# Last layer of a four-layer megakernel: 32 rows per head in zeroed persistent buffers, and four bf16 products ahead of each score tile

## The chip, the core and the metric

The program runs on one core of a Trainium2 chip. A core has five engines with queues of their own: TensorE (PE; its weight loads are shown as PEld), VectorE (DVE), ScalarE (ACT), GpSimd (POOL) and SyncE (SP, which issues the DMAs here). TensorE writes to PSUM, which has eight banks of 128 partitions x 512 fp32; everything else lies in SBUF (128 partitions) or in device memory. Instructions of one engine run in the order in which they were queued; between engines they wait on semaphores.

The metric is the device time of one launch in microseconds (us), as the median of several runs. Before the change it is 3215.15 us over 3 runs (3209.72 to 3215.69).

## What is computed

Four layers follow each other on x of shape (4, 1024, 128). Each does `xn = layernorm(x); x = x + attention(xn) * silu(ffn(xn))`, each with another attention and another feed-forward part. The change touches the attention of the last layer alone: 16 heads of 8 columns, causal softmax attention with learned relative positions.

```python
qx, kx, vx = split_head(x @ Wq.T), split_head(x @ Wk.T), split_head(x @ Wv.T)
ex = rel_embed[ns].reshape(n, NH, HD).transpose(1, 0, 2)        # 256 rows
srel = srel_skew(einsum('bhnd,hmd->bhnm', qx, ex))
...
qk = (einsum('bhnd,bhmd->bhnm', qx, kx) + srel) * inv_dim
mask = 1000000000.0 * triu(ones((n, n)), 1)
atten = softmax(qk - mask, axis=-1)
out = einsum('bhnm,bhmd->bhnd', atten, vx)
return merged_heads(out) @ Wp.T + bp
```

A head has 8 columns, so each score is a sum over 8 products.

## The kernel before

Layers 0 to 2 take the first two thirds of the time and are not edited. The last layer (`layer3`, from line 1725) goes over 4 batches x 4 groups of 4 heads; a group is one pass over 8 query tiles of 128 tokens, in the order `ORDER3 = (7, 0, 6, 1, 5, 2, 4, 3)`. One query tile of one group is a *unit* (128 units). A unit of query tile t has (t+1) x 128 keys and is worked in *score tiles* of up to 512 keys for the 4 heads at once: one score tile when t <= 3, two when t > 3, so 12 a group and 192 in all.

**q and k of a group.** `project3` (line 1962) allocates q as [128, 1 + 1024] and k as [128, 1024] from a pool with two buffers each, sets column 0 of q to zero on POOL (line 1967), and loads the 8 rows of each of the 4 heads by DMA to partitions 32j to 32j+7 (line 1971). The other 24 partitions of each 32 hold nothing. A matrix product whose operands lie on partitions 32j and up uses the row group j of TensorE's array, so four heads lie in four row groups.

**Relative part.** `relative3` (line 1988) multiplies, for two of the four heads and two query tiles, 8 rows of q by 8 rows of the embedding `W["emb"]`, 256 columns wide (line 2000, `pr`). ACT copies the result from PSUM (line 2002, `r`), four DMAs write it to a table in device memory (`flat`, lines 2005 and 2006), and `shear3` (line 2009) reads it back shifted by one column a row (`rel`, lines 2021 to 2027). POOL sets the masked places by affine selects (line 2031). The products run up to seven units ahead of their use, the reads three.

**Scores.** `scores3` (line 2044) is a generator. It first queues the four products of a score tile (line 2064, `score`, one per head, 8 rows each, one PSUM bank each; the four banks are the only buffer of the tag "sc"), then on DVE the scaling, adding of `rel` and row minimum of each head (lines 2072 and 2079, with a read of the accumulator), and after the last score tile of a unit the exponential on ACT (line 2086).

**Weighted sum.** DVE transposes the weights in 32 x 32 blocks (line 1791, `wT`), and `weigh3` (line 2092) multiplies them with `vb`, the values of a group spread so that each of four key blocks has its 8 columns of 32 (line 2100, `po`: 128 rows, 32 columns, 64 or 32 wide, in a column group of the array per head).

**Order.** The main loop (lines 1823 to 1853) takes a turn per score tile, plus four at the end, 196 turns: queue the products of the next score tile, the transposes due, a third of a weighted sum, then DVE's work on the next score tile. At the end of a unit it adds the relative part of a later unit, the load of a later `rel`, a step of whatever lies beside (`ffn3`, the feed-forward part, in the second group of each batch; `begin3`, the layer norm and projections of the next batch, in the third), and at set places `project3` and the values of the next group. A scheduler may then move an instruction among its engine's others as its dependencies allow. PSUM is shared out as "sc" 1 buffer of 4 banks, "tr" 3 buffers of one bank (used by `pr`, the feed-forward part, the projections and transposes) and "o" 1.

fp32 products show as two records each in the profile, so a score tile has 8 MATMUL records.

The loop that the change adds to:

```python
        for x, (n, first) in enumerate(tiles + [(len(units), 0)] * 4):
            next(fill, None)
            if transposes and transposes[0][0] < x:
                transpose(*transposes.pop(0)[1:])
            step()
            next(fill, None)
```

Of the kernel before, what the change touches and what calls it, by code (L numbers as in the profile page):

```python
# [10 lines left out]
F32 = mybir.dt.float32  # L11
BF16 = mybir.dt.bfloat16
# [7 lines left out]
P = 128  # L20
NB = 4
T = 1024
# [65 lines left out]
def drain(gen):  # L88
    for _ in gen:
        pass  # L90
# [1634 lines left out]
def layer3(k, W, x3, out, eps5, ps, first):  # L1725

    nc, tc = k.nc, k.tc
    with ExitStack() as st:
        pool = lambda name, bufs, **kw: st.enter_context(tc.tile_pool(name=name, bufs=bufs, **kw))
        p1, p2, temp, dram = pool("l3", 1), pool("l3d", 2), pool("l3r", 3), pool("rel3", 6, space=DRAM)  # L1740
        vb = p1.tile([P, 32, 4, 4, 8], F32, tag="vb", name="vb")
        nc.gpsimd.memset(vb, 0.0)
        units = [(b, i, t) for b in range(NB) for i in range(4) for t in ORDER3]
        batch, group, flats, rels = {}, {}, {}, {}

        def part(h):

            at, h = divmod(h, 8)
            if at < 4 * NB:
                pair = ORDER3[h // 4 * 4 + h // 2 % 2] // 2  # L1750
                if h % 2 == 0:
                    flats[at, pair] = dram.tile([2, 4, P, 384], F32, tag="flat", name="flat")
                relative3(k, W, temp, ps, flats[at, pair], group[at]["q"], at % 4, pair, h % 2)

        def ahead(n):
            if n < len(units):
                t = units[n][2]
                rels[n] = shear3(k, p2 if t > 3 else p1, flats[n // 8, t // 2], t)

        def stream():  # L1760
            for n, (b, i, t) in enumerate(units):
                yield from scores3(k, p1, p2, ps, group[n // 8], rels.pop(n), t)

        batch[0] = {"qk": first["qk"], "vd": first["vd"], "xnT": p1.tile([P, T], F32, tag="xnT", name="xnT")}
        nc.sync.dma_start(out=batch[0]["xnT"], in_=first["xnT"])
        group[0] = {}
        drain(project3(k, p2, batch[0], 0, group[0]))
        drain(values3(k, p1, batch[0], vb, 0))
        for n in range(7):
            part(n)  # L1770
            if n in (1, 3):
                ahead(n // 2)
        ahead(2)
        beside, project, values = iter(()), iter(()), iter(())
        weights, transposes, weighs, out_of = {}, [], [], {}

        def transpose(n, heads):

            b, i, t = units[n]
            at, pair = n // 8, t // 2  # L1780
            big = t > 3
            if (at, pair) not in weights:
                for w in [w for w in weighs if w[0] == big]:
                    drain(w[1])
                    weighs.remove(w)
                weights[at, pair] = [
                    p1.tile([P, 2, 1024 if big else 512], F32, tag=f"w{'b' if big else 's'}{j}", name="wT") for j in range(4)
                ]
            S = group[at]["S", t]
            for j in heads:  # L1790
                nc.vector.transpose(weights[at, pair][j][:, t % 2, 0 : (t + 1) * P], S[j][:, 0 : (t + 1) * P])  # L1791
            if n % 8 in (2, 3, 6, 7) and heads[-1] == 3:
                weighs.append((big, weigh(n)))

        def weigh(n):
            nonlocal values
            b, i, t = units[n]
            at, pair = n // 8, t // 2
            if n % 8 == 2:
                out_of[at] = ps.tile([P, 8, 32], F32, tag="o", name="po")  # L1800
            o = out_of[at]
            yield from weigh3(k, weights.pop((at, pair)), vb, o, pair)
            if n % 8 == 7:
                drain(values)
                if i == 0:
                    batch[b]["on"] = p1.tile([P, 4, 256], F32, tag="on", name="on")
                finish3(k, p1, ps, o, group[at]["sums"], batch[b]["on"][:, i, :])
                if i == 3:
                    end3(k, W, temp, ps, x3, b, batch[b], out[b])
            yield  # L1810

        def step():

            while weighs:
                if next(weighs[0][1], weighs) is not weighs:
                    return
                weighs.pop(0)

        tiles = [(n, first) for n, (b, i, t) in enumerate(units) for first in range(0, (t + 1) * P, 512)]
        fill = stream()  # L1820
        next(fill)
        next(fill)
        for x, (n, first) in enumerate(tiles + [(len(units), 0)] * 4):
            next(fill, None)
            if transposes and transposes[0][0] < x:
                transpose(*transposes.pop(0)[1:])
            step()
            next(fill, None)
            last = n < len(units) and (x + 1 == len(tiles) or tiles[x + 1][0] > n)
            if not last:  # L1830
                continue
            b, i, t = units[n]
            at, pos = n // 8, n % 8
            transposes += [(x, n, heads) for heads in (((0, 1), (2, 3)) if t > 3 else ((0, 1, 2, 3),))]
            if pos == 0 and at + 1 < 4 * NB:
                group[at + 1] = {}
                project = project3(k, p2, batch[(at + 1) // 4], (at + 1) % 4, group[at + 1])
            if pos == 0 and i == 1:
                beside = ffn3(k, W, p1, temp, ps, batch[b])
            if pos == 3 and i == 2 and b + 1 < NB:  # L1840
                batch[b + 1] = {}
                beside = begin3(k, W, p1, p2, temp, ps, dram, x3, b + 1, eps5, batch[b + 1])
            if pos == 0:

                next(project, None)
            part(n + 7)
            if pos == 2:
                next(project, None)
            if pos == 6 and at + 1 < 4 * NB:
                values = values3(k, p1, batch[(at + 1) // 4], vb, (at + 1) % 4)  # L1850
                next(values)
            next(beside, None)
            ahead(n + 3)
        while weighs:
            step()
# [103 lines left out]
            yield  # L1959


def project3(k, p2, seq, i, group):

    nc = k.nc
    q = p2.tile([P, 1 + T], F32, tag="q", name="q")
    kk = p2.tile([P, T], F32, tag="k", name="k")
    nc.gpsimd.memset(q[:, 0:1], 0.0)
    group.update({"q": q, "k": kk, "sums": p2.tile([P, 4, NT], F32, tag="sums", name="sums")})
    for n, dst in ((0, q[:, 1:]), (1, kk)):
        for j in range(4):  # L1970
            nc.sync.dma_start(out=dst[32 * j : 32 * j + 8], in_=seq["qk"][n, 32 * i + 8 * j : 32 * i + 8 * j + 8])
        yield


def values3(k, p1, seq, vb, i):

    nc = k.nc
    v = p1.tile([P, 32, 32], F32, tag="vr", name="vr")
    for a in range(4):
        rows = slice(32 * a, 32 * a + 32)  # L1980
        nc.sync.dma_start(out=v[rows], in_=seq["vd"].rearrange("(n r) d -> r n d", r=32)[:, :, 32 * i : 32 * i + 32])
    yield
    for a in range(4):
        rows = slice(32 * a, 32 * a + 32)
        nc.gpsimd.tensor_copy(vb[rows, :, :, a, :], v[rows].rearrange("p n (j d) -> p n j d", d=8))


def relative3(k, W, temp, ps, flat, q, i, pair, jp):

    nc = k.nc
    r = temp.tile([P, 2, 2, 256], F32, tag="temp", name="r")
    js = (2 * jp, 2 * jp + 1)
    pr = [ps.tile([P, 2, 256], F32, tag="tr", name="pr") for _ in js]
    for m in range(2):
        for j, to in zip(js, pr):
            at, t = slice(32 * j, 32 * j + 8), 2 * pair + m
            nc.tensor.matmul(to[:, m, :], q[at, t * P : (t + 1) * P], W["emb"][at, i, :], start=True, stop=True)  # L2000
    for n, to in enumerate(pr):
        nc.scalar.copy(r[:, n], to)  # L2002
    rows = flat.rearrange("m j p u -> p j m u")
    for m in range(2):
        nc.sync.dma_start(out=rows[:, 2 * jp : 2 * jp + 2, m, 0:256], in_=r[:, :, m])
        nc.sync.dma_start(out=rows[:, 2 * jp : 2 * jp + 2, m, 256:384], in_=r[:, :, m, 0:P])
# [37 lines left out]
def scores3(k, p1, p2, ps, group, rel, t):  # L2044
# [5 lines left out]
    nc = k.nc  # L2050
    q, kk = group["q"], group["k"]
    n = (t + 1) * P
    at = lambda j: slice(32 * j, 32 * j + 8)
    size = "b" if t > 3 else "s"
    S = [(p2 if t > 3 else p1).tile([P, T if t > 3 else 512], F32, tag=f"S{size}{j}", name="neg") for j in range(4)]
    group["S", t] = S
# [3 lines left out]
    for first in range(0, n, 512):  # L2060
# [7 lines left out]
        for j in range(4):  # L2068

            neg, m = S[j], low[j]  # L2070
# [157 lines left out]
```

## Time and profile before

| | |
|---|---|
| time, median of 3 runs | 3215.15 us (3209.72 to 3215.69) |
| profiled execution, span | 3215.9 us, 50605 instructions |
| PE, DVE, ACT, POOL busy | 72%, 72%, 47%, 36% of the span |
| mean granted TensorE clock | 0.741 of full speed |
| the last layer's scores, `score` L2064 | 1536 records, mean 739 ns |
| products with the embedding, `pr` L2000 | 1024 records, mean 560 ns |
| weighted sums, `po` L2100 | 10240 records, mean 256 ns |
| DVE on the scores, L2079 with `low` / without, L2072 | 448 x 516 ns, 320 x 521 ns, 192 x 416 ns |
| DVE transposes, L1791 | 512 x 754 ns |
| exponentials on ACT, L2086 | 512 x 763 ns |
| copies of `pr` on ACT, L2002 | 256 x 581 ns |
| selects on `rel` on POOL, L2031 | 288 x 638 ns |

The page of the profile names a group of instructions by line, engine, operation and tiles, then its busy time, the mean duration of one, and the idle time of that engine just before them with what ended it. Its first rows give the busy share of the engines in 40 slices of the span, and below these the clock that was granted to TensorE, in tenths of full speed. The last layer lies in the last third of the slices. Matmuls are pipelined and their ends are modelled, so the duration of a single record includes time in which the next one already runs.

### The profile page before, as it was taken

To read this page: it belongs to the slowest core of one execution; us is meant where nothing else is said; L and a number is where in the kernel's file an instruction comes from. 1 tells how busy PE (TensorE), PEld (TensorE's weight loads), DVE (VectorE), ACT (ScalarE), POOL (GpSimd) and SP (SyncE) were. 2 spreads that over 40 slices of the span, in tenths; PEclk is the share of its full clock that TensorE was granted. 3 is DMA by queue.
4 is the path that set the end of the run, shared out by engine and by line. 5 is a ranking of instruction groups with operands and counts; after the bars stand their busy time and mean duration, and the time that the engine had idled before them with its cause. 6 is when DMAs were issued, how large, how long until landed. Compare 5 with 4: busy or idle time off the path is not lost. (4 is left out here: it accounts for less than half of the span.)

```text
span 3215.9 us, 50605 instructions
## 1 busy us (share of the span) xinstructions
PE 2305.2 (72%) x18321; PEld 1320.3 (41%) x18321; DVE 2300.9 (72%) x5538; ACT 1496.1 (47%) x3256; POOL 1155.9 (36%) x1100
## 2 busy tenths in 40 slices
PE   5787778577777766984443772477888888988985
PEld 2555556222232322661110232255555555555553
DVE  5555545878888886657777887547778688688686
ACT  3555544333333333435332561236655665665663
POOL 3334343134444444224468233232222322323322
PEclk9888888588878877995655675566766766767676
DMA  3000000100000000330333446257676677677672
GB/s 87 6 1 1 1 1 1 35 0 0 0 0 7 7 7 7 112 105 7 86 104 100 133 113 139 92 153 209 192 214 202 183 219 217 183 211 209 195 228 68
DMA packets 397310, 308.18 MB, mean 96 GB/s; under 512 B 96368, under 2 KB 379884, under 8 KB 391428
## 3 DMA queue, kind: packets, MB, share of 16 engines
q1 hardware_dynamic: 395908, 300.75, 32.9%
q10 hardware_dynamic: 1152, 4.19, 0.4%
q8 instruction: 144, 2.36, 0.3%
q14 instruction: 106, 0.87, 0.1%
HBM read 162.72 MB, written 141.56 MB: 95 GB/s over the span
## 5 line engine op out<-in xcount | busy, mean ns | idle before, releaser
L2086 ACT ACTIVATE neg<-neg,low 128x640 f32<-128x640 f32 (+7 forms) x512 | 390.0, 763 | 165.1 <-DVE low L2079 165.0
L2031 POOL TENSOR_SCALAR_AFFINE_SELECT rel<-rel 128x512 f32<-128x512 f32 x288 | 180.6, 638 | 577.4 <-DMA rel<-flat 366.4
L1791 DVE STREAM_TRANSPOSE wT<-neg 128x640 f32<-128x640 f32 (+7 forms) x512 | 362.9, 754 | 12.8 <-ACT neg L2086 9.3
L2064 PE MATMUL score<-k,q 8*128 8x512 f32 (+3 forms) x1536 | 294.0, 739 | 86.3 <-DVE low L2079 85.4
L2079 DVE CUSTOM_DVE_ANT_0 neg<-score,rel,low 128x128 f32<-128x128 f32 (+3 forms) x448 | 217.4, 516 | 153.8 <-issue 71.1
L2000 PE MATMUL pr<-emb,q 8*128 8x256 f32 x1024 | 243.9, 560 | 56.1 <-ACT r L2002 29.7
L2100 PE MATMUL po<-wT,vb 128*32 128x64 f32 (+1 forms) x10240 | 236.1, 256 | 35.4 <-issue 24.1
L2100 PEld LDWEIGHTS po<-wT,vb 128*32 128x32 f32 x10240 | 203.3, 138 | 140.3 <-issue 83.9
L2000 PEld LDWEIGHTS pr<-emb,q 8*128 8x128 f32 x1024 | 156.0, 266 | 137.4 <-ACT r L2002 65.7
L2002 ACT COPY r<-pr 128x512 f32<-128x512 f32 x256 | 136.9, 581 | 142.9 <-PE pr L2000 102.6
L2079 DVE CUSTOM_DVE_ANT_0 neg<-score,rel 128x512 f32<-128x512 f32 (+3 forms) x320 | 149.5, 521 | 24.1 <-PE score L2064 8.9
L2064 PEld LDWEIGHTS score<-k,q 8*128 8x128 f32 x1536 | 103.5, 248 | 146.4 <-DVE low L2079 110.5
L835 PE MATMUL pg<-xnT,w 128*128 128x512 f32 x256 | 148.1, 662 | 6.8 <-DVE h L839 3.2
L788 POOL TENSOR_TENSOR prod<-rest,kv 128x2048 f32<-128x2048 f32 x32 | 145.5, 4593 | 18.4 <-ACT rest L778 18.4
L826 PE MATMUL po<-h,w 128*128 128x512 f32 x256 | 131.5, 635 | 27.0 <-DVE h L839 27.0
L214 PE MATMUL pt<-ident,three 128*24 128x128 bf16 x64 | 9.2, 295 | 197.6 <-DVE three L211 197.6
L837 PE MATMUL pu<-xin,w 128*128 128x512 f32 x256 | 140.9, 634 | 13.7 <-DVE h L839 7.7
L838 ACT ACTIVATE h<-pg 128x512 f32<-128x512 f32 x128 | 75.9, 595 | 156.5 <-PE pg L835 153.1
L1084 PE MATMUL ph<-xin,upT 128*128 128x512 bf16 (+1 forms) x128 | 69.8, 575 | 65.3 <-DVE xin L1078 63.9
L431 PE MATMUL px<-hT,xbcT 128*128 128x512 f32 x256 | 115.4, 595 | 0.0
L1489 PE MATMUL read<-kt,const_sb 128*128 128x128 f32 x256 | 50.7, 370 | 90.2 <-POOL kt L1484 90.2
L2072 DVE TENSOR_SCALAR_CACHE_REDUCE neg<-score 128x384 f32<-128x384 f32 (+2 forms) x192 | 79.9, 416 | 47.7 <-PE score L2064 46.2
(631 smaller groups left out, 5671.7 us busy)
## 6 DMA issues: line engine op xcount, KB each, us to landing
flat<-r SPq DMA_DIRECT2D x256, 256.0 KB
rel<-flat SPq DMA_DIRECT2D x112, 512.0 KB
flat<-r SPq DMA_DIRECT2D x256, 128.0 KB
rel<-flat SPq DMA_DIRECT2D x96, 256.0 KB
kt<-kd SPq DMA_DIRECT2D x16, 512.0 KB
qt<-qd SPq DMA_DIRECT2D x16, 512.0 KB
kdc<-kdd SPq DMA_DIRECT2D x16, 512.0 KB
ktc<-ktd SPq DMA_DIRECT2D x16, 512.0 KB
```

The source lines that it names most:

```text
L788: nc.gpsimd.tensor_tensor(prod, attn.rearrange("p (t h g) -> p t h g", t=4, g=16)[:, t].unsqueeze(2).to_broadcast(each), kv[:, t, 1, :].re ...
L826: nc.tensor.matmul(po, W["w2"][:, e, c, :], h[:, c, :], start=(e == 0 and c == 0), stop=(e == 7 and c == 1))
L835: nc.tensor.matmul(pg, W["w1"][:, e, c * P : (c + 1) * P], xnT, start=True, stop=True)
L837: nc.tensor.matmul(pu, W["w3"][:, e, c * P : (c + 1) * P], xin, start=True, stop=True)
L1791: nc.vector.transpose(weights[at, pair][j][:, t % 2, 0 : (t + 1) * P], S[j][:, 0 : (t + 1) * P])
L2000: nc.tensor.matmul(to[:, m, :], q[at, t * P : (t + 1) * P], W["emb"][at, i, :], start=True, stop=True)
L2002: nc.scalar.copy(r[:, n], to)
L2031: nc.gpsimd.affine_select(out=rel[:, :, slot(back), :], in_=rel[:, :, slot(0), :], compare_op=op, fill=fill, base=0, pattern=[[0, 4], [-si ...
L2064: nc.tensor.matmul(sc[:, j, 0 : last - first], q[at(j), 1 + t * P : 1 + n], kk[at(j), first:last], start=True, stop=True)
L2079: nc.vector.tensor_tensor_reduce(out=neg[:, begin:last], in0=sc[:, j, begin - first : last - first], in1=rel[:, j, slot : slot + (last - b ...
L2086: nc.scalar.activation(neg[:, 0:n], neg[:, 0:n], AF.Exp, bias=here, scale=-1.0, accum_out=group["sums"][:, j, t : t + 1])
L2100: nc.tensor.matmul(o[32 * j : 32 * j + 32, 2 * pair + m.start : 2 * pair + 2, :], vb[:, kb, j].rearrange("p a d -> p (a d)"), weights[j][: ...
```

## The change

Three things change, all in the last layer.

First, q and k of the groups are no longer taken from a rotating pool. Two pairs of buffers are allocated once and set to zero as a whole, one pair on DVE and one on POOL, and a group uses the pair of its parity. `project3` loads the same 8 rows per head into them by the same DMAs, and its memset of q's first column is dropped, since that column stays zero.

Second, the products of `relative3` and `scores3` take 32 rows per head where they took 8. The 24 added rows of q and k are zero (those of `W["emb"]` are zero as well), so the sums stay what they were.

Third, at the start of each turn of the main loop `keep_warm(4)` queues four bf16 products of the identity (128 x 128, `k.ident16`) with a tile of ones (128 x 512) into one PSUM buffer of the tag "tr". Nothing reads the result. `tc.keep_in_program_order` marks them for the scheduler. In the order as built, a group of four stands ahead of nearly every score tile, some with products of `relative3` or part of a weighted sum between, and each of the four has a weight load of its own.

```diff
         p1, p2, temp, dram = pool("l3", 1), pool("l3d", 2), pool("l3r", 3), pool("rel3", 6, space=DRAM)
+        pairs = []
+        for n in range(2):
+            q, kk = p1.tile([P, 1 + T], F32, tag=f"q{n}", name="q"), p1.tile([P, T], F32, tag=f"k{n}", name="k")
+            for a in (q, kk):
+                (nc.gpsimd if n else nc.vector).memset(a, 0.0)
+            pairs.append((q, kk))
         vb = p1.tile([P, 32, 4, 4, 8], F32, tag="vb", name="vb")
+        ones = p1.tile([P, 512], BF16, tag="ones16", name="ones")
+        nc.vector.memset(ones, 1.0)
+
+        def keep_warm(count):
+
+            spare = ps.tile([P, 512], F32, tag="tr", name="spare")
+            for _ in range(count):
+                tc.keep_in_program_order(nc.tensor.matmul(spare, k.ident16, ones, start=True, stop=True))
+
...
-        drain(project3(k, p2, batch[0], 0, group[0]))
+        drain(project3(k, p2, pairs[0], batch[0], 0, group[0]))
...
         for x, (n, first) in enumerate(tiles + [(len(units), 0)] * 4):
+            keep_warm(4)
             next(fill, None)
...
-                project = project3(k, p2, batch[(at + 1) // 4], (at + 1) % 4, group[at + 1])
+                project = project3(k, p2, pairs[(at + 1) % 2], batch[(at + 1) // 4], (at + 1) % 4, group[at + 1])
...
-def project3(k, p2, seq, i, group):
+def project3(k, p2, pairs, seq, i, group):
 
     nc = k.nc
-    q = p2.tile([P, 1 + T], F32, tag="q", name="q")
-    kk = p2.tile([P, T], F32, tag="k", name="k")
-    nc.gpsimd.memset(q[:, 0:1], 0.0)
+    q, kk = pairs
...
         for j, to in zip(js, pr):
-            at, t = slice(32 * j, 32 * j + 8), 2 * pair + m
+            at, t = slice(32 * j, 32 * j + 32), 2 * pair + m
             nc.tensor.matmul(to[:, m, :], q[at, t * P : (t + 1) * P], W["emb"][at, i, :], start=True, stop=True)
...
-    at = lambda j: slice(32 * j, 32 * j + 8)
+    at = lambda j: slice(32 * j, 32 * j + 32)
```

## The prediction

> **What bounds the kernel now.** I read the stretch of the last layer first (busy time by window), then what VectorE (DVE) waits for in it, then single windows, because only the last layer is edited. The columns are the stretch in us, its length, busy us and instructions (x) of PE, PEld, DVE, ACT, POOL, then the granted TensorE clock, the DMA share and GB/s.
>
> ```profile
> 2173.00:3193.00 1020.00, 853.55 (x13084) 541.21 (x13088) 801.22 (x2526) 625.95 (x1476) 289.30 (x412) 0.69 0.69 198
> ```
>
> These are 1020 of the 3215.9 us. PE is busy 84% of them, DVE 79%, and the clock is 0.69, so TensorE does at a reduced rate what would take less at full rate. Neither engine is full; the two wait for each other. The waits of DVE in that stretch:
>
> ```profile
> DVE neg L2079 <- issue: 76.9, 28, 7.5
> DVE neg L2079 <- PE score L2064: 68.5, 51, 3.8
> DVE neg L2072 <- PE score L2064: 28.1, 14, 4.6
> DVE wT L1791 <- ACT neg L2086: 9.3, 19, 3.0
> DVE neg L2079 <- POOL rel L2031: 9.2, 4, 4.6
> ```
>
> The unnamed "issue" waits are score waits too. In the longest one DVE stands 7.47 us while PE, at half clock, does the feed-forward part and then the scores, whose end releases it:
>
> ```profile
> 2772.56 1.05 PE L1957 MATMUL po<-downT,h 128*128 128x128 f32 x4
> 2773.54 0.91 PE L2064 MATMUL score<-k,q 8*128 8x384 f32 x2
> 2774.38 1.16 PE L1957 MATMUL po<-downT,h 128*128 128x128 f32 x8
> 2775.46 0.92 PE L2064 MATMUL score<-k,q 8*128 8x384 f32 x6
> ...
> 2776.54 0.62 DVE L2079 CUSTOM_DVE_ANT_0 neg<-score,rel,low 128x384 f32<-128x384 f32 x1 [7.47 <-issue]
> ```
>
> So DVE waits for scores 76.9 + 68.5 + 28.1 = 173.5 us in 93 waits, 1.87 us each, over 189 score tiles (1512 records, 8 a tile). That is all the change can win; PE in turn waits for DVE 84.2 us in 69 waits before scores.
>
> Why is the clock low while PE is busy? In the windows below PE is full or nearly so. Lines one and two count all instructions; lines three and four are the first window again with the scores (L2064) alone and the products pr (L2000) alone (PE and PEld only); line five is a window whose PE records are all weighted sums po (L2100, likewise alone), line six the window after it, with all instructions:
>
> ```profile
> 2831.49:2834.90 3.41, 3.41 (x17) 1.90 (x17) 3.35 (x10) 2.84 (x11) 3.27 (x4) 0.50 0.93 238
> 2834.90:2838.31 3.41, 3.13 (x16) 1.76 (x14) 3.41 (x15) 1.66 (x3) 2.49 (x4) 0.50 0.71 237
> 2831.49:2834.90 3.41, 2.72 (x8) 1.06 (x8) 0.50 0.93 238
> 2831.49:2834.90 3.41, 1.52 (x7) 1.13 (x9) 0.50 0.93 238
> 2660.83:2664.24 3.41, 3.41 (x139) 3.41 (x134) 0.50 1.13 368
> 2664.24:2667.65 3.41, 3.13 (x138) 2.28 (x130) 2.37 (x9) 1.84 (x4) 0.00 (x0) 1.00 0.96 224
> ```
>
> A full window of scores and pr (8 of 32 rows of each row group) leaves the clock at 0.50; a full window of po (128 rows) is followed by 1.00. I went over all 306 clock windows of the layer in the trace's records this way. Counting busy time times occupied rows (score 4 x 8/128 = 0.25, pr 2 x 8/128 = 0.125, the rest 1) times the clock, "over 0.4 of the window" names the next window's clock in 95% of them; counting all rows alike does so in 67%. That is an inference from the records. The weights vb of po are zero in 24 of their 32 columns per row and still count, so zeros need not be lost.
>
> The Trainium skill ("TensorE: Matmul & The Clock Gate", Part 1) says instead that any busy window of about 3.4 us releases the clock and an idle one throttles it. This case's full 3.41 us window at 0.50 disagrees. By that rule the 84% busy PE would have nothing to gain and the sum would be the cost of the new products alone.
>
> **The change, part by part.** *Clock.* PE time at full clock is 853.55 x 0.69 = 589 us of the 1020, or 3.12 us a tile against 4.52 now. Is it reached? With 32 rows a score counts 1 and a pr 0.5. Per tile at full clock: scores 288.4 us x 0.69 / 189 = 1.05, pr 226.5 x 0.69 / 189 x 0.5 = 0.41, po 233.2 x 0.69 / 189 = 0.85 (busy times of the lines in the stretch), plus the new products 0.86 (below): 3.17 us in a tile of some 5.3, 0.60 of the time where 0.4 keeps it. I take a mean clock of 0.96, the rest for windows in which PE starves. If zero rows do not count, it is 0.26 + 0.10 + 0.85 + 0.86 = 2.07 of 5.3 = 0.39, on the edge.
>
> *Rows.* 32 rows instead of 8 add no instruction. Do more rows take longer? The lines compare a score tile of 8 rows with 128-row products at full clock, and with itself at half clock:
>
> ```profile
> 2631.53 1.14 PE L2064 MATMUL score<-k,q 8*128 8x512 f32 x8
> 2637.71 2.09 PE L2064 MATMUL score<-k,q 8*128 8x512 f32 x8
> 2792.36 0.59 PE L1947 MATMUL pgu<-xnT,gateT 128*128 128x256 f32 x2
> 2792.79 0.59 PE L1947 MATMUL pgu<-xnT,upT 128*128 128x256 f32 x2
> ```
>
> Two queued pgu records of 256 columns start 0.43 us before the next two, so 0.215 a record, 0.43 for 512 columns. The four row groups of a score run side by side, two records after each other: 2 x 0.43 and a tail of 0.28 make 1.14. So 8 rows and 128 go at one pace, and I take 0; bounds 0 and, from the tail, 0.28 x 196 = 55 us if all of it grew with the rows.
>
> *Four products a tile.* 196 turns x 4 = 784, 756 in the 189 tiles. A bf16 record of 512 columns lasts at least 0.376 us alone at full clock (ph), as an fp32 record of 256 columns does (pr, 0.374); queued, the latter come every 0.215 us as pgu shows. So 0.86 us a tile at full clock, 1.72 at half; weight loads of 0.095 us lie beside the matmul before. They stand directly ahead of the scores, behind no data of DVE. Where PE is waiting for DVE they cost nothing: 69 of 189 tiles, with 84.2 / 69 = 1.2 us each, enough cover for 0.86. Without that cover they are 0.86 in line.
>
> At clock 0.96 PE has (613.5 + 756 x 0.215 / 0.96 = 169.3) / 189 = 4.14 us a tile with them, 3.25 without. Against 4.52 a wait shrinks by 0.38 where they are in line (64%) and 1.27 where covered (36%): 0.70 on the mean, x 93 waits = -65 us. Bounds: -35 (all in line) and -118 (all covered).
>
> *Their PSUM buffer.* They take the tag "tr" (3 buffers) and may wait for ACT's copy of pr (0.58 us), and pr comes round sooner behind its predecessors. PE waits 27.9 us before pr for that copy now, its weight loads 61.3. Bounds: 0 and +61 (as much again); I take +8, nearer to nothing because a spare's buffer was last used a tile or more ago, longer than the copy takes, and most such waits sit beside DVE work. Behind a waiting product stand the scores, and behind these DVE.
>
> *Switching between row groups, column groups and the full array.* Two more per tile. In the trace po at 2632.59 starts before the scores at 2631.53 + 1.14 end, so no gap; upper bound 0.376 - 0.215 = 0.16 us x 2 x 196 = 63 us. I take 0. The Trainium skill ("TensorEngine Tiling (Array Packing)", Key Properties) says that changing the tiling mode drains TensorE, which speaks against this change; it gives no time, and by it the sum would move toward that upper bound.
>
> *Persistent q and k.* Removed: POOL's 16 memsets of q[:, 0:1] (0.10 us), for which POOL stood 53.0 us behind scores, with the selects on rel queued after them; DVE waits 9.2 us for these selects, so 0 to -9. The DMAs of q still wait for the same readers on SP's queue, eight DMAs a group as before, and move past nothing. Added once: two whole memsets on POOL ahead of vb's (vb, 4096 wide, took 3.51, so two of some 1024 are 1.8) and three on DVE, which is idle for 18 us then. q's load no longer stands behind vb's memset. Bounds -3 to +2. For both together I take -1.
>
> Sum: 3215.9 - 65 + 8 + 0 - 1 = 3157.9 on the profiled span. The median is 3215.15, the runs 3209.72 to 3215.69, so the span stands 0.75 above the median; I say **3158**.
>
> **Rivals.** *Partial clock.* Zero rows do not count, and 0.39 lies at the threshold. With 0.85, PE has (589 + 162.5) / 0.85 / 189 = 4.68 us a tile in line and 3.67 covered: -0.64 x 0.16 + 0.36 x 0.85 = 0.20 us x 93 = -19, +8 -1: 3204. For it: the products with empty rows may not count. Against: vb's zeros.
>
> *The products stay in line at a low clock (slower).* The clock stays near 0.69 because the gate hardly counts the new rows and products. PE then needs 853.55 + 162.5 / 0.69 = 1089 us, more than the 1020, and each tile gets 0.86 / 0.69 = 1.25 us of it. Let through on the 93 late tiles at 64% it is 74 us, on all 189 at 64% 151 us; nearer the first, since the others have slack: 3215.9 + 77 + 8 - 1 = 3300. It decides below the clock c where 0.64 x 3.98 / c + 0.36 x 3.12 / c = 4.52, that is 0.81 (3.98 and 3.12 are the tile's PE time at full clock with and without the products). For it: the gate counted 8 rows for little. Against: full-row windows did raise the clock.
>
> *More cover than I count.* All late tiles covered give -118, all score waits gone -173.5 (3042, where DVE's own 801 us rule); halfway -146, so 3070. For it: PE, done sooner, waits for DVE more often. Against: the DMA share is 0.69 already and rises as the stretch shrinks, and the selects on rel wait for its transfers.
>
> **How the numbers follow.** First case 0.60 (3158; own range 3105 to 3190), partial clock 0.19 (3204), slower 0.17 (3300), more cover 0.04 (3070). The 8-in-10 range goes from 3085 to 3228: below, 3215.9 - 118 - 9 and a little of the last case; above, the partial clock with half the buffer's upper bound in place of its 8, 3204 + 23; the slower case is left out with 0.17. Within 0.2% is 6.4 us, about what a measurement tells. Of the partial clock 0.11 is faster, 0.05 the same, 0.03 slower: faster 0.60 + 0.04 + 0.11 = 0.75, same 0.05, slower 0.17 + 0.03 = 0.20.
>
> **What would show it.** Right: a clock over 0.9 in the last layer, score tiles of 512 columns near 1.14 us throughout, DVE's share over 83%, its score waits near 110 us. Wrong: a clock under 0.81, records of the new products 0.43 us apart, or waits of PE for ACT before them; the sum is wrong in the cover if the clock rises and the score waits of DVE stay.

## The result, and the profile after

The changed kernel is slower. Its median is 3257.64 us (4 runs, 3245.84 to 3263.62) against 3215.42 us for the kernel before in the same comparison: a ratio of 1.012, 95% interval 1.0094 to 1.0146, some 39 us more. The prediction said 3158 us and held 3085 to 3228 us for likely.

The whole-layer window of after comes first, over the same stretch as before (columns: stretch, length, busy us and instructions of PE, PEld, DVE, ACT, POOL, then granted clock, DMA share, GB/s). The layer no longer fits into that stretch; the second line is the layer from its first to its last reduction.

```profile
2173.00:3193.00 1020.00, 860.28 (x13286) 465.22 (x13282) 760.78 (x2413) 586.81 (x1408) 278.91 (x388) 0.91 0.67 195
2170.00:3229.00 1059.00, 890.89 (x13800) 478.62 (x13804) 796.31 (x2523) 607.13 (x1461) 286.64 (x398) 0.91 0.65 191
```

The clock rose, from 0.69 to 0.91 (the forecast was 0.96). But PE is busy for as long as before (860 us of the 1020, it was 854): the new products took all that the clock gave. DVE's share of the stretch fell from 79% to 75%, since it now waits longer. The groups of TensorE's instructions on the page of after (records, busy us, mean ns, then idle time before them and who ended it):

```profile
L2078 PE MATMUL score<-k,q 32*128 32x512 f32 (+3 forms) x1536 | 224.6, 594 | 110.1 <-DVE low L2093 107.6
L1755 PE MATMUL spare<-ones,ident 128*128 128x512 bf16 x784 | 231.2, 422 | 4.5 <-DVE on L2135 2.9
L2114 PE MATMUL po<-wT,vb 128*32 128x64 f32 (+1 forms) x10240 | 188.8, 223 | 15.2 <-issue 15.0
```

A score record went from 739 to 594 ns and a weighted-sum record from 256 to 223 ns, which goes the way of the faster clock. The 784 new products were all executed and they hardly wait themselves (4.5 us idle before all of them). What DVE waits for in the layer of after, from 2190 to 3232 us (us in total, times, longest):

```profile
DVE neg L2093 <- PE score L2078: 120.6, 62, 10.5
DVE neg L2086 <- PE score L2078: 60.3, 15, 8.0
DVE neg L2093 <- issue: 18.9, 11, 5.9
```

These are 199.8 us in 88 waits where it was 173.5 us in 93. There are not more waits, they are longer: 2.27 us each against 1.87, with 15 waits of 4 us each before the first reduction of a long row (L2086), which had 14 of 2 us.

Where in the layer? The mean time of a unit can be taken from DVE's records, from the end of its last reduction to the end of the one before it, and added up by group (four batches each):

```
mean us of a group      first   second (feed-forward)   third   fourth   t=6 in the second
before                   63.2          71.7              61.2     61.8        16.8
after                    61.8          83.0              61.6     61.3        25.4
```

So the second groups lost 4 x 11.3 = 45 us, nearly all in one unit, t = 6, and the other twelve gained 6 us between them. That gain lies in the very first group of the layer, which is about 10 us shorter; the other eleven are together some 4 us longer. So the faster clock bought next to nothing in these groups, and in four something else went wrong. The timeline of after in such a unit shows what (start, duration, engine, instruction, in brackets the idle time before it and its releaser):

```profile
2779.24 1.14 PE L2078 MATMUL score<-k,q 32*128 32x512 f32 x6 [0.15 <-DVE low L2093]
2781.97 0.70 PE L1963 MATMUL pgu<-xnT,gateT 128*128 128x256 f32 x2 [1.60 <-ACT r L2016]
...
2783.89 1.12 PE L2078 MATMUL score<-k,q 32*128 32x512 f32 x2
...
2788.00 1.03 PE L1755 MATMUL spare<-ones,ident 128*128 128x512 bf16 x4
2788.96 1.83 PE L2114 MATMUL po<-wT,vb 128*32 128x64 f32 x126
...
2797.08 0.91 PE L2078 MATMUL score<-k,q 32*128 32x384 f32 x2
...
2798.91 1.03 PE L1755 MATMUL spare<-ones,ident 128*128 128x512 bf16 x4
2799.87 0.92 PE L2078 MATMUL score<-k,q 32*128 32x384 f32 x6
...
2785.14 0.42 DVE L2086 TENSOR_SCALAR_CACHE_REDUCE neg<-score 128x256 f32<-128x256 f32 x1 [5.96 <-PE score L2078]
2800.85 0.62 DVE L2093 CUSTOM_DVE_ANT_0 neg<-score,rel,low 128x384 f32<-128x384 f32 x1 [5.85 <-PE score L2078]
```

Three heads' scores start at 2779.24, but the last two records of the tile come only at 2783.89. Four feed-forward products stand between, and the first of them waits 1.60 us for ACT's copy of `pr`, that is, for a buffer of the ring "tr". DVE stands 5.96 us. Then 13.2 us of other work pass on PE (rest of the feed-forward step, spare products, a weighted sum, `pr`, a second feed-forward step) before the next score tile starts at 2797.08, and DVE stands again. PE is never idle for long here; the work stands in a bad order.

### The profile page after: what moved, and what is told of

It reads as the page before. It is cut to its first block, busy times and chain, and to the rows that moved or that the text cites. A ratio compares the mean times of both kernels' runs of the same rounds, so it can differ in the third digit from the quotient of the medians.

```text
span 3254.0 us, 52149 instructions
## 1 busy us (share of the span) xinstructions
PE 2351.2 (72%) x19105; PEld 1259.0 (39%) x19105; DVE 2300.0 (71%) x5541; ACT 1479.8 (45%) x3246; POOL 1154.7 (35%) x1086
## 5 line engine op out<-in xcount | busy, mean ns | idle before, releaser
L2078 PE MATMUL score<-k,q 32*128 32x512 f32 (+3 forms) x1536 | 224.6, 594 | 110.1 <-DVE low L2093 107.6
L1755 PE MATMUL spare<-ones,ident 128*128 128x512 bf16 x784 | 231.2, 422 | 4.5 <-DVE on L2135 2.9
L2114 PE MATMUL po<-wT,vb 128*32 128x64 f32 (+1 forms) x10240 | 188.8, 223 | 15.2 <-issue 15.0
L2014 PE MATMUL pr<-emb,q 32*128 32x256 f32 x1024 | 180.7, 428 | 24.7 <-ACT r L2016 13.4
L2114 PEld LDWEIGHTS po<-wT,vb 128*32 128x32 f32 x10240 | 156.2, 114 | 107.7 <-issue 104.1
L2078 PEld LDWEIGHTS score<-k,q 32*128 32x128 f32 x1536 | 75.1, 200 | 181.0 <-DVE low L2093 133.0
L2014 PEld LDWEIGHTS pr<-emb,q 32*128 32x128 f32 x1024 | 106.7, 198 | 94.8 <-issue 48.0
L2086 DVE TENSOR_SCALAR_CACHE_REDUCE neg<-score 128x384 f32<-128x384 f32 (+2 forms) x192 | 79.9, 416 | 72.2 <-PE score L2078 72.2
L1755 PEld LDWEIGHTS <-ident 128*128 128x128 bf16 x784 | 67.7, 104 | 134.4 <-issue 90.8
```

The source lines that it names most:

```text
L1755: tc.keep_in_program_order(nc.tensor.matmul(spare, k.ident16, ones, start=True, stop=True))
L2078: nc.tensor.matmul(sc[:, j, 0 : last - first], q[at(j), 1 + t * P : 1 + n], kk[at(j), first:last], start=True, stop=True)
L2114: nc.tensor.matmul(o[32 * j : 32 * j + 32, 2 * pair + m.start : 2 * pair + 2, :], vb[:, kb, j].rearrange("p a d -> p (a d)"), weights[j][: ...
```

## The experiments

Each ratio is to runs of the kernel before in the same comparison, about 3220 us, so 0.001 is 3.2 us. Edits are against the changed kernel unless said otherwise.

### The rows alone, and the products alone

The first takes out `keep_warm` and leaves rows and persistent buffers; the second leaves the products and takes 8 rows again.

```diff
-            keep_warm(4)
```

> 32 rows and the zeroed pairs, without the added products; the instructions stand on TensorE as in the kernel before. If the clock gate counts zero rows as rows: clock of the last layer 0.78 to 0.88 (0.44 of the full-speed window filled, threshold 0.4) and, if score waits follow the PE time, 3150 to 3190 us. If zero rows do not count: clock 0.69 and 3215. If the clock rises and the time stays at 3215, the clock is not what the waits hang on.

```diff
-            at, t = slice(32 * j, 32 * j + 32), 2 * pair + m
+            at, t = slice(32 * j, 32 * j + 8), 2 * pair + m
...
-    at = lambda j: slice(32 * j, 32 * j + 32)
+    at = lambda j: slice(32 * j, 32 * j + 8)
```

> The four added products with 8 rows per head as before; TensorE's order as in the changed kernel. Theory A (the order that the added products bring, in the groups with the feed-forward part, costs the time, whatever the clock): second groups near 83 us again, 3250 to 3300. Theory B (the time of the products on PE costs it): 3250 to 3300 too, but spread over all groups. Clock 0.75 to 0.85 if zero rows were counted in the changed kernel, 0.91 again if they were not.

Rows alone: 3193.52 us, ratio 0.9916 (0.9891 to 0.9941), faster than both kernels. Products alone: 3303.89 us, ratio 1.0256 (1.0235 to 1.0277). The layer's window of each:

```profile
2173.00:3164.00 991.00, 793.58 (x13044) 498.94 (x13048) 801.36 (x2525) 625.05 (x1473) 287.88 (x398) 0.76 0.70 205
```

```profile
2172.00:3271.00 1099.00, 986.99 (x13632) 534.60 (x13755) 796.81 (x2523) 608.36 (x1461) 287.51 (x398) 0.78 0.63 184
```

With the rows alone TensorE has the same instructions as before, in the same order but for a few weighted-sum products, and it is busy for a smaller share (80% against 84%), yet its clock is 0.76 instead of 0.69. Clock and time both stay just short of what was expected of zero rows that count (0.78 to 0.88, 3150 to 3190 us).

This run also holds the persistent buffers. The cleaner pair is the products alone against the changed kernel: both have the buffers and the products, and they differ in the rows only. There the clock is 0.78 with 8 rows and 0.91 with 32, and the 24 rows are worth 0.0136, some 44 us, with an uncertainty of about 11. The added rows hold zeros only, so zero rows count. The products alone cost 82 us, a little more than both theories had expected, so the loss of the change lies in the products.

### One short product instead of four long ones

This keeps the place, the ring's buffer and the mark for the scheduler, and takes most of the TensorE time away.

```diff
-                tc.keep_in_program_order(nc.tensor.matmul(spare, k.ident16, ones, start=True, stop=True))
+                tc.keep_in_program_order(nc.tensor.matmul(spare[:, 0:32], k.ident16, ones[:, 0:32], start=True, stop=True))
...
-            keep_warm(4)
+            keep_warm(1)
```

> 32 rows; one product of 32 columns a turn instead of four of 512, pinned and with a buffer of the ring as before: the products' PE time is gone (about 0.05 us a turn), their place and their buffer stay. Theory A (place and buffer): 3235 to 3260, second groups over 78 us. Theory B (PE time): 3150 to 3200, second groups under 72.

3234.91 us, ratio 1.0051 (1.0032 to 1.007): 0.0135 or 43 us above the rows alone, at the lower end of theory A, for products that last 0.2 us and hardly wait (group of this kernel):

```profile
L1755 PE MATMUL spare<-ones,ident 128*128 128x32 bf16 x196 | 38.7, 198 | 5.5 <-ACT r L2016 5.1 <-DVE s L2150 0.3
```

The unit t = 6 of the second groups takes 25.9 us here, as in the changed kernel, and 15.3 with the rows alone. So most of this loss cannot be the work of the four long products. The unit is not late in quite the same way, though: here TensorE also stands idle before the feed-forward part's down products, for POOL's `h` (us in total, times, longest). With the rows alone this wait is 2.5 us, in the changed kernel 5.8.

```profile
PE po L1973 <- POOL h L1969: 30.2, 15, 4.1
```

### Is it the fixed order, the feed-forward part, or its place?

First the short product without `keep_in_program_order`, then the four long ones without it:

```diff
-                tc.keep_in_program_order(nc.tensor.matmul(spare[:, 0:32], k.ident16, ones[:, 0:32], start=True, stop=True))
+                nc.tensor.matmul(spare[:, 0:32], k.ident16, ones[:, 0:32], start=True, stop=True)
```

> As the short products (one of 32 columns a turn, 32 rows), with the buffer of the ring but not pinned to their place. TensorE's order near the feed-forward part is then nearly that of the kernel before. Theory A, the order: second groups 68 to 73 us, 3190 to 3205. Rival, the ring buffer itself: second groups near 80 us again, 3225 to 3245.

```diff
-                tc.keep_in_program_order(nc.tensor.matmul(spare, k.ident16, ones, start=True, stop=True))
+                nc.tensor.matmul(spare, k.ident16, ones, start=True, stop=True)
```

> The changed kernel with the four products not pinned; they keep the ring buffer and their PE time. The order near the feed-forward part stays that of the changed kernel. Theory A: second groups 80 to 85 us, 3245 to 3265. If the pin itself costs the time: under 3230.

The free short product: 3218.66 us, ratio 0.9997 (0.998 to 1.0015). Its second groups are back at 68.3 us (rows alone 68.9), but the three other kinds of group are longer by 6.1 us together, so 26 us of the 43 remain, in other places than before. That lies between the two expectations. Here the free products do wait for ACT's copies, 17.5 us in 7 waits. The free long products: 3258.33 us, ratio 1.0111 (1.0089 to 1.0133), as with the order fixed. With four products the mark for the scheduler is not the cause.

No products in the second groups at all:

```diff
-            keep_warm(4)
+            if n < len(units) and units[n][1] != 1:
+                keep_warm(4)
```

> The changed kernel without the added products in the second group of each batch (48 of 196 turns). Theory A: second groups back to 72 us or below, the others as in the changed kernel, 3195 to 3215. Theory B: 3257 less about 48 x 0.9 = 43 us times the share in line (64%), 3225 to 3235, second groups near 76.

3243.39 us, ratio 1.007 (1.0051 to 1.0089). That wins 16 us of the 39, less than both expectations said; the second groups are still 77.9 us long and their t = 6 takes 23.9 us, against 68.9 and 15.3 with the rows alone. No added product runs in these groups before their last two microseconds, and none takes a buffer there. What is left of the products is the order in which TensorE's other instructions were built, and it is nearly that of the changed kernel around t = 6 (timeline of this run):

```profile
2491.80 1.13 PE L2079 MATMUL score<-k,q 32*128 32x512 f32 x6 [0.22 <-DVE low L2094]
...
2496.94 2.07 PE L2079 MATMUL score<-k,q 32*128 32x512 f32 x2
...
2504.15 1.14 PE L2115 MATMUL po<-wT,vb 128*32 128x64 f32 x64
...
2511.61 0.91 PE L2079 MATMUL score<-k,q 32*128 32x384 f32 x2
```

The first tile is split again by feed-forward products, and the rest of that step, a weighted sum, `pr` and a second step stand before the second tile, 19.8 us after the first. So most of the loss of the second groups, 9.0 of 14.1 us a group against the rows alone, needs neither the products' time nor a buffer of the ring in these groups; it comes with the built order.

Then four runs that move the feed-forward steps: on every second unit, with the products and with the rows alone, and one unit earlier, likewise with both.

```diff
-            next(beside, None)
+            if i != 1 or pos % 2 == 0:
+                next(beside, None)
```

> The changed kernel; in the second groups a step of the feed-forward part follows each second unit (all long ones: t = 7, 6, 5, 4) instead of the first four units. Theory A (two steps of the feed-forward part stand before the scores of t = 6 once the added products hold TensorE's order): t = 6 of the second groups falls from 25.4 to 16 to 19 us, second groups to 70 to 77 us, 3215 to 3235. Rival (the added products' own time and waits in these groups): second groups stay above 79 us, 3245 to 3260.

> 32 rows without the added products, the feed-forward steps after each second unit as in the run before. Theory A: second groups fall from 68.9 to 62 to 67 us, 3165 to 3190, faster than both kernels. Rival (the feed-forward part costs the same wherever it stands): 3190 to 3200.

```diff
-            if pos == 0 and i == 1:
+            if pos == 7 and i == 0:
...
-            next(beside, None)
+            if pos or i != 1:
+                next(beside, None)
```

> The changed kernel with the first feed-forward step queued one unit earlier (after t = 3 of the first group instead of after t = 7 of the second), the other three as they were. TensorE then has the first step ahead of the second score tile of t = 7, as the kernel before had it, and no step ahead of the first score tile of t = 6. Theory A (the added products keep the scheduler from moving that step ahead, and the scores of t = 6 then wait behind two steps): t = 6 of the second groups from 25.4 to 15 to 18 us, t = 7 up by 0 to 3, second groups 72 to 76, time 3215 to 3235. Rival (a step costs the same wherever it stands, as the spread steps did): no less than 3245.

> 32 rows without the added products, and the first feed-forward step one unit earlier, as in the first kernel of this call. The scheduler had moved that step ahead by itself, so theory A expects little: second groups 66 to 70 us, 3185 to 3200. Below 3185 it would be the best kernel here; above 3210, a step in the wrong place costs without any added product.

Spread: 1.0226 (1.0203 to 1.0248) with products, 1.0065 (1.0048 to 1.0082) with rows alone. Earlier: 1.0104 (1.0074 to 1.0133) and 0.9971 (0.9957 to 0.9986). None helped: with the products the spread steps cost more and the earlier one changes nothing clear of noise, and with the rows alone both were slower (by 48 and 18 us). These four runs show no better place for the feed-forward steps. In the earlier variant t = 6 shrinks from 25.4 to 19.0 us, and t = 7 and t = 5 grow.

In the order as built there is a difference that these runs don't touch. With the rows alone the scheduler has cut the first feed-forward step into pieces and put these ahead of earlier score tiles, while in the changed kernel most of that step and all of the next stand around the two tiles of t = 6. So I forced something like that with the rows alone:

```diff
-            next(beside, None)
+            if i == 1:
+                with tc.issue_after(k.score):
+                    next(beside, None)
+            else:
+                next(beside, None)
...
-            nc.tensor.matmul(
+            k.score = nc.tensor.matmul(
...
-            )
+            ).ins
```

> 32 rows, no added products, no added buffer; in the second groups the feed-forward steps are only made to stand behind the scores that were queued before them, as they do in the changed kernel: six of its products before the first score tile of t = 6, two steps' worth before the second. Theory A, the order alone: t = 6 of the second groups 22 to 26 us (15.3 with the rows alone), second groups 76 to 82, 3220 to 3245. Rival, the products or their buffer are needed for the loss: t = 6 at 15 to 18 us, 3190 to 3205.

3206.57 us, ratio 0.9954 (0.9937 to 0.997): 0.0038 or 12 us above the rows alone, with 18.7 us for t = 6. The time lies just above the rival's range and far below that of theory A. The built order is not that of the changed kernel: the rest of the first step and the whole next one do stand between the two tiles of t = 6, but no feed-forward product splits the first tile, and the weighted sum stands ahead of it. So this part of the order gives some 12 us, with an uncertainty of about 10, and the run does not test the whole order.

### The same place without the ring's buffer

Here the product writes into the score tile's own bank, ahead of the scores that write over it. It stands directly ahead of the scores, and it is not marked for the scheduler. With one short product the rest of TensorE's order is close to that of the rows alone (a few hundred of the 10240 weighted-sum records, some tens of `pr` and six of the feed-forward part stand a tile or two elsewhere); with long ones it differs more. Edit against the rows alone (one short product; two or four long ones; the tile of ones is allocated as in the change):

```diff
         sc = ps.tile([P, 4, 512], F32, tag="sc", name="score")
+        nc.tensor.matmul(sc[:, 0, 0:32], k.ident16, k.ones16[:, 0:32], start=True, stop=True)
```

> 32 rows, and ahead of each score tile one 32-column bf16 product into the score tile's own first bank, which the scores then write over: no buffer of the ring is taken and TensorE's order is that of the rows alone with 196 products put in. Theory (the loss of the pinned short product is the ring's buffer and the order that it leaves behind): the rows' time, 0.9916 of the kernel before, plus 196 products of at most 0.2 us: 3190 to 3225 us, and the tile t=6 of the second groups takes at most 17 us. Rival (a product directly ahead of the scores costs this wherever its output goes): about 3235 us, as the pinned one in the ring. Leaves out nothing of the result.

```diff
         sc = ps.tile([P, 4, 512], F32, tag="sc", name="score")
+        for j in range(4):
+            nc.tensor.matmul(sc[:, j, :], k.ident16, k.ones16, start=True, stop=True)
```

> 32 rows, and ahead of each score tile four 512-column bf16 products into the score tile's own four banks, which the scores then write over: the changed kernel without the ring's buffer and with TensorE's order that of the rows alone. A product can start only when the score tile is free, so nearly all of its time is in line where the scores are waited for. Theory (clock gain kept, products in line): the clock of the last layer is about 0.91; 3193 - 68 for the clock (the inferred part beyond the rows) + 784 x 0.215 = 169 us, all of it: 3294; with the part of 54 per cent that eight against four products gave, 3217. Range 3217 to 3294. Rival (the prediction's price holds when order and ring are left alone: 64 per cent of 0.86 us at 93 tiles = 53 us): 3178 us.

> As the kernel with four products in the score tile's own banks, with two of them. Theory (the price goes with the number of products, 84 us if all of two products is in line, 46 at 54 per cent; the clock rises less, to about 0.84, half the gain): 3193 - 34 + 46 to 84 = 3205 to 3243 us, between the rows alone and the four. Rival (the gate needs only a little more, the clock is already near 0.9 with two): clock over 0.88 and 3171 to 3209.

Short: 3196.38 us, ratio 0.9919 (0.9901 to 0.9937), the time of the rows alone (0.9916). The unit t = 6 takes 17.2 us, a little over the 17 expected and far from 25.9. Its group on the page, with a wait for the score buffer that the scores had before:

```profile
L2071 PE MATMUL score<-ones,ident 128*128 128x32 bf16 x192 | 37.4, 195 | 119.1 <-DVE low L2088 110.5
```

So a product ahead of each score tile, two more changes of the array's use included, costs +1 us, with an uncertainty of about 10. The short product of the ring differs from this one in the buffer, in the mark and in its place at the start of the turn. Without the mark 26 us of its 43 remain, so the mark is 17 of them, and the buffer and the place together are the rest; these two were not told apart.

Two long: 3256.01 us, 1.0101 (1.0083 to 1.0119), 13 us above the expected range. Four long: 3296.38 us, 1.023 (1.0208 to 1.0252), 2 us above the range, whose upper end took all of their time as in line. The layer's window with two, then with four:

```profile
2173.00:3228.00 1055.00, 841.98 (x13348) 477.93 (x13466) 799.14 (x2523) 619.45 (x1466) 288.13 (x398) 0.82 0.67 191
```

```profile
2173.00:3278.00 1105.00, 906.14 (x13733) 497.78 (x13864) 804.13 (x2523) 622.59 (x1468) 287.02 (x398) 0.87 0.63 183
```

The clock goes 0.77, 0.82, 0.87 (short, two, four), and the time lies 59 and 100 us above that with the short one. Here a product can start only when the score buffer is free, so nearly all of it is in line, and it costs more than its clock brings.

The run with four says something on the second groups as well. It has the same four products ahead of each tile as the changed kernel, but not in the ring, and its t = 6 there takes 13.2 us, less than the 15.3 us of the rows alone. Its two tiles start 8.7 us apart (the scores alone):

```profile
2526.41 1.14 PE L2074 MATMUL score<-k,q 32*128 32x512 f32 x8
...
2535.07 0.93 PE L2074 MATMUL score<-k,q 32*128 32x384 f32 x8
```

So the long unit t = 6 goes with products in the ring and the order that was built with them, and not with the work of four products.

### Eight products

```diff
-            keep_warm(4)
+            keep_warm(8)
```

> Eight products a turn instead of four: 784 more of 0.215 us, 169 us of PE time at full clock, in the same places. If 64% of it stands in line with the scores, as predicted for the four: +108 us, 3365; if PE's waits cover most of it: +40 or less; if every one delays a score: +169, 3425. Clock 0.93 to 0.97 in the last layer.

3353.23 us, ratio 1.0402 (1.0377 to 1.0427), 0.0282 or 91 us above the changed kernel, and the layer's clock:

```profile
2174.00:3327.00 1153.00, 1001.90 (x14367) 542.95 (x14494) 795.51 (x2526) 612.40 (x1461) 289.43 (x398) 0.94 0.61 175
```

From 0.91 to 0.94 the clock gives little, so this is close to the bare price of the second 784 products: 91 of 784 x 0.215 = 169 us, 54% of their TensorE time at full clock. The expectation was a little dearer than that.

## Why the prediction was wrong

The measured steps are: rows alone -27 us (0.9916), the short product in the ring +43 (to 1.0051), four long ones instead of the short one +22 (to 1.012); together +38. The prediction's sum was -65 for the clock with the products' price in it, +8 for their buffer and -1: together -58. So two steps of it failed. Clock, products and persistent buffers together brought -27 + 22 = -5 us where -66 was forecast, and the PSUM buffer cost 43 where 8 was forecast: 61 and 35 of the 96 us between forecast and result.

The +22 is a price less a clock gain. With the 91 us of the run with eight as the price, the gain from 0.76 to 0.91 is 91 - 22 = 69 us. That split is inferred: it takes the first four products to cost what the second four did, and it puts down to clock and price what the order on TensorE, which differs between these two kernels too, may have added.

*Clock: right in kind, about a fifth too large.* Forecast 0.96 and 1.27 us x 93 = -118 us; got 0.91 and, by that split, about -27 - 69 = -96. That the gate counts occupied rows, zeros too, was an inference and is now shown by the two pairs of runs that differ in the rows. By the rule of the Trainium skill that the prediction set against it ("TensorE: Matmul & The Clock Gate", Part 1), any busy window releases the clock, so the rows alone had no reason to leave 0.69; they got 0.76 with a less busy PE. The prediction's count of windows is less one-sided than it reads: a recount over 299 windows gives 94% for occupied rows at 0.4, and 78% for all rows alike at the threshold that suits that count best, 0.68.

*Four products a tile: by that split the most mis-sized term.* The prediction charged them 0.64 x 0.89 us (4.14 - 3.25) on the "93 late tiles" only, +53 us, because the others had slack. The second four cost 91 us, and the first four are taken to cost as much. A likely reason is that the slack was not there to be spent: a tile whose scores come in time may do so by less than 0.86 us, and a product that fills a gap on PE pushes back `pr` and weighted sums, which had used that gap. Which tiles pay was not measured.

*Their PSUM buffer: the step whose reasoning failed.* The prediction took +8 out of 0 to +61, "because a spare's buffer was last used a tile or more ago". That reasoning asked whether the new products would wait, and in the changed kernel they hardly do: 1.1 us for ACT, 5.1 us with one short product. It didn't ask what becomes of the others: the three buffers carry `pr` and the feed-forward part, and with 196 more turns of the ring the scheduler built another order. The loss is 43 us (short product in the ring against rows alone), and with the mark on the products it lies nearly all in the second groups. In the changed kernel, in the run with short products and in the run without products in the second groups the same work stands between the two tiles of t = 6: the down products of one feed-forward step, a weighted sum, `pr`, and most of the next step. That unit then takes 25.4, 25.9 and 23.9 us; it takes 15.3 with the rows alone and 13.2 with four products that stay out of the ring, where only most of one step stands there. So for the second groups the built order is the cause, as far as these comparisons go. What stays open is why the scheduler built it, what part of the 43 us is TensorE's 30.2 us of standing for POOL's `h`, and what the 26 us are that the free short product loses in the other groups.

For comparison, the same work with the rows alone, around the second score tile of t = 6 (timeline):

```profile
2746.26 0.71 PE L2068 MATMUL score<-k,q 32*128 32x512 f32 x3
...
2754.41 0.79 PE L1963 MATMUL po<-downT,h 128*128 128x128 f32 x4
2755.12 0.91 PE L2068 MATMUL score<-k,q 32*128 32x384 f32 x2
2756.11 1.16 PE L1963 MATMUL po<-downT,h 128*128 128x128 f32 x8
2757.19 0.92 PE L2068 MATMUL score<-k,q 32*128 32x384 f32 x6
...
2758.27 0.62 DVE L2083 CUSTOM_DVE_ANT_0 neg<-score,rel,low 128x384 f32<-128x384 f32 x1 [4.54 <-issue]
```

One feed-forward step stands between the two tiles (scores at 2746.26 and 2755.12, 8.9 us apart), and DVE's long wait there is 4.54 us. In the changed kernel the two tiles start 17.8 us apart (2779.24 and 2797.08).

*Rows and switching at nothing: held as far as measured.* A queued score tile of 32 rows and 512 columns takes 1.14 us (at 2771.40 with the short product in the ring), as one of 8 rows did at full clock before. For switching, the short product in the score tile's bank gives +1 us, with an uncertainty of about 10, where the prediction's upper bound was 63. The persistent buffers were not tried alone; they are part of the -27.

*The rivals and the signs.* The slower rival had the right sign but the wrong cause: it needed a clock below 0.81, and the clock rose to 0.91. That its 3300 us is what the products alone take (3303.89 us) is luck: it reckoned with a clock near 0.69 and 8 us for the buffer, and that run had 0.78 and the built order of the changed kernel. Of the signs that the prediction named for being right, the clock over 0.9 came; DVE's share (75%, not over 83%) and its score waits (199.8 us, not near 110) did not. A clock that rises while the score waits of DVE stay was its sign that the cover was wrong, and that is what happened.

## What to carry to other kernels

A filler that nobody reads can be paid for twice: its own time on an in-order engine, here 54% of it in line for the second four with the clock already high, and the order that the rest of the work gets when the filler takes buffers of a ring that this work turns on. Ask of a new user of a ring what the old users will do, and not only whether it waits itself; then look at the order as built. And take a change apart first: the rows alone, with no added instruction in the loop, were worth 27 us (3193.52 us, the fastest kernel here), and the products took that and more.

## What the runs showed of the hardware

The granted clock follows the occupied rows of the array, and not only the busy time. With 8 rows of 32 in use the last layer got 0.69, and with 32, of which 24 hold zeros, 0.76, while PE's busy share fell from 84% to 80%. With the four products beside them, in the same order on TensorE, it was 0.78 and 0.91.

A faster clock was worth less than the TensorE time that it saved. With the rows alone PE's busy time in the layer fell by 853.55 - 793.58 = 60 us, but DVE's score waits only by 28 us (173.5 to 145.8) and the span by 3215.9 - 3188.6 = 27 us; PE's waits for DVE before scores rose from 84.2 to 105.9 us.
